# A deformable-convolution stack with a mixture-of-experts block: six gather buffers instead of ten, fourteen sample buffers instead of eight

## The chip, the cores and the metric

The kernel runs on one core of a Trainium2 chip. The metric is the device time of one execution in microseconds. TensorE is called PE here (PEld is its weight load), VectorE DVE, ScalarE ACT, GpSimd POOL and SyncE SP.

## What is computed

The input `x` is (4, 256, 64, 64) in float32. It is normalised over the channels and goes through three modulated deformable 3x3 convolutions with ReLU; the result is added to `x`. Each pixel's 256 channels then form a token that goes, normalised, through a mixture of eight experts (256 to 512 to 256, GELU), of which the two with the highest gate probability are taken, and is added again. One deformable convolution is, cut to what matters here:

```python
om = conv3x3(x, w_off) + b_off                 # 27 values per pixel
off, mask = om[:, :18].reshape(B, 9, 2, H, W), sigmoid(om[:, 18:])
ys, xs = gy + base_y + off[:, :, 0], gx + base_x + off[:, :, 1]
sampled = bilinear(x, ys, xs) * mask           # 4 corners per pixel and tap
out = einsum('bikhw,oik->bohw', sampled, w) + b
x = relu(out)
```

Each pixel and each of nine taps so reads four neighbouring pixels at a place that only the data know.

## The kernel before

**Work and stages.** Three layers times four images are twelve stages (`self.stages` in `run`). A stage has eight blocks of 512 pixels (`NB`), a block nine taps (`K`), and a tap four samples: a sample here is 128 pixels (one per partition) by 256 channels for one tap. There are 12 x 8 x 9 x 4 = 3456 samples. `main_block` loops over taps and, within a tap, over two pairs of samples.

**A sample's way.** For each layer and image a table lies in DRAM whose rows hold a pixel and the one below it, so that two neighbouring rows, 4 KB together, are the four corners. `samples` does four things for each sample, one on each engine:

- L503, POOL: an indirect DMA gathers 128 table rows of 4 KB into a tile `g` of pool `gat` (4 KB per partition). The row numbers `idx` come from a plan made earlier (`off_block`).
- L509, DVE: blends the two columns, in place in `g`.
- L514, DVE: blends the two rows into a tile `s` of pool `smp` (1 KB per partition). After it `g` is free.
- L517, ACT: scales `s` in place with the mask and weight.

`turn` then takes a pair of samples: PE transposes the two `s` into PSUM (L532), after which they are free, and ACT copies the result to `sT` (L535). After two pairs `finish` multiplies `sT` with the tap's weights and accumulates in `acc` (L555). `LAG = 2` keeps `turn` two pairs behind `samples` in the order in which instructions are recorded.

**Order and rings.** The recorded order goes through a scheduler which fixes each engine's order at build time; engines then run in that order and wait on semaphores. A tile of a pool can be written when all users of an earlier tile in the same buffer are done. So `gat`'s buffer count bounds how far POOL's gathers run ahead of DVE's second blend, and `smp`'s how far DVE's blends run ahead of PE's transposes. In the build of before, a gather waits for a blend of an earlier sample (the buffer) and for an earlier DMA of the software queue.

**Work beside.** Between taps other work is woven in on all engines. `off_block` makes offsets and plans (L357, L366, L371, L387 to L427). `pre_block` normalises the input of a later image (L442, L462, L467). `rows_done` and `store_table` write the next layer's table (L328, L338). `tokens`, `route` and `invert` prepare the FFN (L599 to L788: gate, ranks, slots; `at` and `num` at L777 and L779). `expert` runs an FFN tile: POOL fetches weights `w` (L800) and tokens `zt` (L812), PE transposes (L840) and multiplies (L856, L874), ACT copies (L844) and applies GELU (L866), `products` writes `y` with DVE (L892). `combine_fetch` and `combine` gather the experts' results `gy` (L915) and add them to `ta` on DVE (L930); `give` transposes and stores (L948 to L956). An FFN tile's steps are spaced by a pace of 5, 5, 2, 1.5 and 0 taps for the five groups of tokens.

**Other users of the gather buffers.** While the kernel starts, `room` takes the blocks `xc` and `h` of `pre_block` from the pool `gat`. The last FFN group takes its `gy` from it as well, after the last gather (`combine_fetch`).

Of the kernel before, what the change touches and what calls it, by code (L numbers as in the profile page):

```python
# [34 lines left out]
FT_LOG = 8  # L35
FT = 1 << FT_LOG
FU = FT // P
GB = 10
LAG = 2
LEAST = 2.0**-30  # L40
WINN = CC * (RPB + 2) * W
# [41 lines left out]
class Group:  # L83


    def __init__(self, b, n0, n1):
        self.b, self.n0, self.n1 = b, n0, n1
        self.nm = f"{b}_{n0}"
        self.M = (n1 - n0) * TPB

        self.NF = 2 * self.M * P // FT + E - 1


        self.half = (self.NF + 1) // 2
        self.zt, self.acc, self.gy, self.sums, self.py = {}, [], [], [], None
        self.order = [s // 2 + s % 2 * self.half for s in range(self.NF)]
# [21 lines left out]
class Weave:  # L118
# [3 lines left out]
    def __init__(self, ctx, tc, ins, out):  # L122
        nc = self.nc = tc.nc
        self.tc = tc
        self.ins = ins
        self.x = ins["x"].rearrange("b (c p) h w -> b p c (h w)", p=P)
        self.out_v = out.rearrange("b (c p) h w -> b p c (h w)", p=P)
        self.B = self.x.shape[0]

        def pool(name, bufs, **kw):  # L130
            return ctx.enter_context(tc.tile_pool(name=name, bufs=bufs, **kw))

        self.cst = pool("cst", 1)
        self.dram = pool("dram", 1, space=bass.MemoryType.DRAM)
        self.wkp = pool("wkp", 1)
        self.plan = pool("plan", 19)
        self.win = pool("win", 3)
        self.wt = pool("wt", 2)
        self.small = pool("small", 1)
        self.big = pool("big", 2)  # L140
        self.ffn = pool("ffn", 2)
        self.rt = pool("rt", 1)
        self.rt2 = pool("rt2", 2)
        self.gyp = pool("gyp", 4)
        self.smT = pool("smT", 2)
        self.smp = pool("smp", 8)
        self.gat = pool("gat", GB)
        self.ps = pool("ps", 3, space=bass.MemoryType.PSUM)
        self.ps1 = pool("ps1", 1, space=bass.MemoryType.PSUM)

        self.routes, self.tiles, self.sums = Lane(), Lane(), Lane()
        self.side, self.plans_side = [], []
        self.last = self.gathered = self.turned = None
        self.starting, self.draining, self.later = True, False, []
        self.pend, self.pairs = None, []
# [980 lines left out]
```

## Time and profile before

| | |
|---|---|
| median of 9 runs | 7635.78 us (7607.57 to 7649.76) |
| the profiled execution | 7654.8 us |
| its span | 7653.1 us, 88985 instructions |
| granted PE clock, mean | 0.937 |
| first and last gather issued | 94.0 us, 7194.3 us |
| bytes moved | 2223.73 MB, 291 GB/s in the mean |
| software queue (gathers, FFN fetches) | 1947.35 MB, 72.3% of 16 DMA engines' span |
| hardware queue (SP's loads and stores) | 270.69 MB, 10.7% |

The span is the time from the first to the last recorded instruction of the profiled execution. A row of the groups or the timeline names the line, the engine, the operation and the tiles, output first (`s<-g,cf`). A wait is idle time of an engine before an instruction, put down to what ended it; "issue" means that nothing in the profile ended it, and "remote" that the releaser was not found.

### The profile page before, as it was taken

The page shows a single profiled execution, that of the slowest core. Times are in us where ns is not written, and L with a number is a line of the kernel's source. Part 1 is how long each engine was busy: PE and PEld are TensorE (multiplying, and loading weights), DVE is VectorE, ACT ScalarE, POOL GpSimd, SP SyncE. Part 2 cuts the span into 40 slices and gives each one's busy share as a digit, 9 for nine tenths or more (in the row PEclk, how much of TensorE's full clock was granted, in tenths as well). Part 3 has the DMA queues.
Part 4 walks back from the last instruction along what each step waited for, and adds up shares of the span by engine and source line. Part 5 has one row for each costly group of instructions (what it writes and reads, how often), then busy time and mean ns, then how long its engine had stood idle before and what let it go on. Part 6 is the DMA issues. An engine that isn't in the chain of part 4 may idle for free.

```text
span 7653.1 us, 88985 instructions
## 1 busy us (share of the span) xinstructions
PE 6480.1 (85%) x26500; PEld 3640.5 (48%) x26500; DVE 4952.0 (65%) x11467; ACT 3266.2 (43%) x7141; POOL 4468.3 (58%) x4245
## 2 busy tenths in 40 slices
PE   7887888888898888889987888888888788977887
PEld 3443333334444444455554444544444455644565
DVE  6776777778886566567777556656767554667421
ACT  3444444444544444445443444444444333444322
POOL 4654666656666556556556656655655555566543
PEclk8999999999999999999998999999998899999888
DMA  8987999989999888888888889888887777888644
GB/s 270 337 315 269 345 324 338 344 324 354 353 344 315 291 298 294 285 299 314 302 296 306 285 280 317 298 290 296 294 301 281 253 256 240 275 293 287 202 134 125
DMA packets 800319, 2223.73 MB, mean 291 GB/s; under 512 B 104728, under 2 KB 302872, under 8 KB 794080
## 3 DMA queue, kind: packets, MB, share of 16 engines
q0 software_dynamic: 551200, 1947.35, 72.3%
q1 hardware_dynamic: 248640, 270.69, 10.7%
q8 instruction: 215, 3.52, 0.2%
q14 instruction: 264, 2.16, 0.1%
HBM read 2160.68 MB, written 196.40 MB: 308 GB/s over the span
## 4 chain that ended last, share of the span: by engine, by line
PE 67%; ACT 10%; another core or an unknown queue 8%; issue 7%; DVE 4%; DMA 2%; POOL 1%; SPq 0%; ACTq 0%; POOLq 0%; DVEq 0%
PE acc L555 33%; PE tp L532 10%; PE ph L856 7%; PE py L874 7%; PE po L357 6%; ACT sT L535 4%; ACT s L517 3%; DVE g L509 1%; PE pm L371 1%; DVE s L514 1%; ACT hT L866 1%; PE ftp L840 1%; PE lp_tok L618 1%; ACT win L577 1%
## 5 line engine op out<-in xcount | busy, mean ns | idle before, releaser
L503 POOL DMA_INDIRECT g<-tab,idx x3456 | 3679.4, 1065 | 2468.9 <-DVE s L514 1106.6
L555 PE MATMUL acc<-sT,wk 128*128 128x512 f32 x6912 | 3502.9, 622 | 272.0 <-ACT sT L535 147.2
L509 DVE SCALAR_TENSOR_TENSOR g<-g,cf 128x512 f32<-128x512 f32 x3456 | 2557.9, 742 | 261.5 <-DMA g<-tab,idx 243.2
L514 DVE SCALAR_TENSOR_TENSOR s<-g,cf 128x256 f32<-128x256 f32 x3456 | 1661.9, 483 | 1409.4 <-PE tp L532 746.3
L535 ACT COPY sT<-tp 128x512 f32<-128x512 f32 x1728 | 1001.9, 585 | 2416.6 <-PE tp L532 1576.9
L555 PEld LDWEIGHTS acc<-sT,wk 128*128 128x128 f32 x6912 | 1200.4, 198 | 1130.1 <-issue 831.3
L517 ACT ACTIVATE s<-s,cf 128x256 f32<-128x256 f32 x3456 | 1628.7, 508 | 242.7 <-DVE s L514 156.4
L532 PEld LDWEIGHTS tp<-ident,s 128*128 128x128 f32 x6912 | 897.2, 147 | 1715.1 <-issue 953.1
L532 PE MATMUL tp<-ident,s 128*128 128x128 f32 x6912 | 1291.1, 288 | 484.5 <-ACT s L517 269.7
L874 PE MATMUL py<-w,hT 128*128 128x256 f32 x2608 | 687.0, 403 | 139.7 <-ACT hT L866 84.7
L856 PE MATMUL ph<-fzT,w 128*128 128x256 f32 x2608 | 721.1, 411 | 67.3 <-ACT fzT L844 29.7
L874 PEld LDWEIGHTS py<-w,hT 128*128 128x128 f32 x2608 | 494.4, 200 | 282.0 <-ACT hT L866 123.1
L856 PEld LDWEIGHTS ph<-fzT,w 128*128 128x128 f32 x2608 | 507.9, 206 | 204.5 <-issue 68.2
L866 ACT ACTIVATE hT<-ph,w 128x256 f32<-128x256 f32 x652 | 281.9, 471 | 634.4 <-PE ph L856 372.9
L812 POOL DMA_INDIRECT zt<-z,tok x326 | 333.6, 1023 | 171.3 <-issue 87.7
L800 POOL DMA_INDIRECT w<-in_W,wrow x163 | 177.1, 1087 | 416.0 <-ACT sT L535 172.6
L357 PE MATMUL po<-win,wo 128*32 128x504 f32 (+1 forms) x2304 | 364.6, 609 | 6.7 <-ACT win L301 3.6
L892 DVE TENSOR_TENSOR y<-py,w 128x512 f32<-128x512 f32 x163 | 111.9, 686 | 377.8 <-PE py L874 314.0
L915 POOL DMA_INDIRECT gy<-ys,slots x256 | 254.5, 994 | 108.0 <-issue 71.8
L930 DVE SCALAR_TENSOR_TENSOR ta<-gy,cw,ta 128x256 f32<-128x256 f32 x256 | 120.4, 479 | 128.6 <-DMA gy<-ys,slots 76.0
L357 PE MATMUL po<-win_pre,wo 128*32 128x504 f32 (+1 forms) x1152 | 187.7, 628 | 2.0 <-ACT om L366 2.0
L366 ACT ACTIVATE om<-po,bo 128x512 f32<-128x512 f32 x96 | 66.0, 687 | 255.3 <-PE po L357 170.0
(154 smaller groups left out, 2968.5 us busy)
## 6 DMA issues: line engine op xcount, KB each, us to landing
tab<-hv SPq DMA_DIRECT2D x512, 128.0 KB
g<-tab,idx POOLq DMA_INDIRECT x3456
ys<-y SPq DMA_DIRECT2D x163, 256.0 KB
tab<-h_pre SPq DMA_DIRECT2D x128, 256.0 KB
wk<-in_conv_w SPq DMA_DIRECT2D x99, 256.0 KB
xc_pre<-in_x SPq DMA_DIRECT2D x32, 512.0 KB
xr_tok<-in_x SPq DMA_DIRECT2D x32, 512.0 KB
t<-t_tok SPq DMA_DIRECT2D x32, 512.0 KB
```

The source lines that it names most:

```text
L357: nc.tensor.matmul(po[g * Q : (g + 1) * Q, :].rearrange("q (r w) -> q r w", w=W)[:, :, x0:x1], lhsT=self.wo[l][:, 3 * ky + kx, c, :], rhs= ...
L503: self.gathered = nc.gpsimd.indirect_dma_start(out=g.rearrange("p x s f -> p (x s f)"), out_offset=None, in_=self.table(*self.stages[i]), ...
L509: nc.vector.scalar_tensor_tensor(g[:, :, 0, :], g[:, :, 1, :], cf[:, j, 0:1], g[:, :, 0, :], ALU.mult, ALU.add,)
L514: self.last = nc.vector.scalar_tensor_tensor(s, g[:, 1, 0, :], cf[:, j, 1:2], g[:, 0, 0, :], ALU.mult, ALU.add)
L517: nc.scalar.activation(s, s, AF.Copy, scale=cf[:, j, 2:3])
L532: self.turned = nc.tensor.transpose(tp[:, c, u * P : (u + 1) * P], ss[u][:, c * P : (c + 1) * P], self.ident)
L535: nc.scalar.copy(self.sT[:, :, t0 * P : (t0 + 2) * P], tp)
L555: nc.tensor.matmul(acc[:, o, :], lhsT=self.wk[k][:, c, o * P : (o + 1) * P], rhs=sT[:, c, :], start=(k == 0 and c == 0), stop=(k == K - 1 ...
L812: self.nc.gpsimd.indirect_dma_start(out=zt, out_offset=None, in_=grp.zd, in_offset=bass.IndirectOffsetOnAxis(ap=grp.tok[:, j : j + 1], axi ...
L856: nc.tensor.matmul(ph[:, h, :], lhsT=w1[:, o : o + P], rhs=zT[:, c, :], start=(c == 0), stop=(c == CC - 1),)
L866: nc.scalar.activation(ht[:, h, :], ph[:, h, :], AF.Gelu, bias=w1[:, k : k + 1])
L874: nc.tensor.matmul(py[:, u, :], lhsT=hT[h // 2][:, h % 2, u * P : (u + 1) * P], rhs=w2[:, h * C : (h + 1) * C], start=(h == 0), stop=(h == ...
```

## The change

The pool of gather tiles has six buffers instead of ten, and the pool of blended samples fourteen instead of eight. Per partition that is 16 KB less and 6 KB more. Nothing else is edited; the scheduler makes each engine's order anew.

```diff
-GB = 10
+GB = 6
...
-        self.smp = pool("smp", 8)
+        self.smp = pool("smp", 14)
         self.gat = pool("gat", GB)
```

## The prediction

> **What bounds the kernel now.** I read the busy times first, then the waits, then the instruction rows of single stretches.
>
> ```profile
> PE 6480.1 (85%) x26500; PEld 3640.5 (48%) x26500; DVE 4952.0 (65%) x11467; ACT 3266.2 (43%) x7141; POOL 4468.3 (58%) x4245
> ```
>
> PE is the busiest engine. The span of 7653.1 us is its 6480 us and about 1170 us of idle time; only a change that shortens this idle time or adds to it moves the end. Two of the waits look as if the change would act on them (columns: who waited for whom, us in total, times, longest):
>
> ```profile
> POOL g L503 <- DVE s L514: 1106.6, 646, 14.6
> DVE s L514 <- PE tp L532: 746.3, 616, 8.9
> DVE s L514 <- remote: 232.6, 101, 12.4
> ```
>
> They form a chain of full rings. POOL cannot gather because all ten `g` are held; DVE cannot free one because its blend needs a free `s`; the `s` are held until PE has transposed them. But these are waits of the engines that feed PE, and a feeder that waits for its customer is early. PE's own waits say what PE lacks:
>
> ```profile
> PE tp L532 <- ACT s L517: 269.7, 245, 15.4
> PE acc L555 <- ACT sT L535: 147.2, 167, 5.9
> ...
> ACT s L517 <- DVE s L514: 156.4, 167, 9.0
> ```
>
> PE waits for ACT, which scales a sample in place (L517) and copies the transposed pair (L535). ACT in turn waited for DVE's blend only 156.4 us.
>
> I then paired the rows by count: gathers, both blending operations, the scaling and the transposes run through the samples in one order, so the k-th row of L503, L509, L514 and L517 and the k-th two of L532 are the same sample. A gather's landing I took from the software queue's packets: each gather has 128 packets of 4 KB, and the end of the last is its landing, to a few tenths of a us. Three things come out.
>
> (a) A gather takes 5.2 us in the median from issue to landing (7.0 at the 95th percentile). Up to 6000 us the median gather finds ten buffers held at its issue, of which 3 to 4 are in flight and some six have landed and wait.
> (b) From landing to its blend a sample lies 10.2 us in the median, and from blend to transposition another 12.0 us; six blended samples are in stock when PE transposes one.
> (c) Of PE's idle time (1158 us in gaps over 0.1 us) 467 us stand before a transposition whose sample was blended before PE went idle, and 15.6 us, in ten gaps, before one that was not; of these 7.4 us are the first samples of all, which no buffer helps.
>
> So through most of the kernel the supply of samples is not what PE waits for. Two stretches are different. At the first gathers the rings are empty (start in us, duration, engine, line, operation, idle time before it):
>
> ```profile
> 93.98 1.02 POOL L503 DMA_INDIRECT g<-tab,idx  x1 [58.67 <-DMA tab<-h_pre]
> ...
> 96.59 0.94 POOL L503 DMA_INDIRECT g<-tab,idx  x1 [0.30 <-issue]
> 97.84 0.94 POOL L503 DMA_INDIRECT g<-tab,idx  x1 [0.30 <-issue]
> 98.00 0.75 DVE L509 SCALAR_TENSOR_TENSOR g<-g,cf 128x512 f32<-128x512 f32 x1 [10.49 <-DMA g<-tab,idx]
> 98.79 0.48 DVE L514 SCALAR_TENSOR_TENSOR s<-g,cf 128x256 f32<-128x256 f32 x1
> ...
> 104.31 0.75 DVE L509 SCALAR_TENSOR_TENSOR g<-g,cf 128x512 f32<-128x512 f32 x1
> ```
>
> The first gather is blended 4.0 us after its issue, the fourth (97.84) after 6.5 us. The other is 6000 to 7200 us, with an FFN tile every 1.5 to 2 taps (DVE's waits in that window):
>
> ```profile
> DVE g L509 <- DMA g<-tab,idx: 230.1, 75, 10.3
> ...
> DVE s L514 <- PE tp L532: 21.7, 9, 8.9
> ```
>
> Nearly all of DVE's 243.2 us for gathers lies there, and a full `s` ring hardly occurs. POOL is held there by the weight fetch at L800 (172.6 us behind `ACT sT L535` over the kernel), not by `g`: the median gather finds five buffers held, and only 29% more than six.
>
> **The change, part by part.** No instruction is added or removed in the computation. In the built programs the order of samples is the same, and few instructions change places: 31 on POOL, 91 on DVE, 442 on ACT (by six places at most), 531 on PE, nearly all of them in the second half of each engine's order.
>
> *Six g.* A buffer's turn is the landing (5.2 us), two blends (0.742 + 0.483 us by L509 and L514) and about 0.35 us until POOL starts again: 6.8 us, so six buffers allow one sample each 1.13 us. With the 7.0 us latency it is 8.6 / 6 = 1.43 us. POOL issues at best each 1.25 us (the rows at 96.59 and 97.84), and the kernel consumes one each 2.05 us ((7194.3 - 94.0) / 3456). Six is therefore enough in the steady state, by a factor of 1.8, and too few only for a fast catch-up on a loaded queue.
>
> One step finer: I hold every gather of before back to the end of the blend six earlier plus 0.3 us, with its own latency, and compare its landing with the time at which DVE blended it. The mean gather moves 6.2 us later, and 111 of 3456 blends become late, in 59 episodes whose longest lateness adds up to 67 us. Of this, 27 us are one episode at 5914 us, where POOL sits behind the first fetches of an FFN group; there the new order puts two or three gathers ahead of those fetches. The other 58 episodes are at most 2.8 us each, and in the twenty longest the samples had 2 to 19 us between blend and transposition. So 0 to +27 us reach PE; I take +12, between, since the reordering mends part. With five buffers the same count gives 613 late blends: six stands near an edge.
>
> *Fourteen s.* DVE's 979 us (746.3 + 232.6) of waiting for a free `s` shrink, but they stand on no path to PE by (b) and (c). What it can save: of the 15.6 us in (c) the 8 us after the start, and the part of ACT's 156.4 us that PE feels. ACT is idle 4387 us (span less busy), and PE's gaps behind a scaling that started late are 402 us, 9% of that; 9% of 156 is 14 us. Ends are 0 and 156; I take 14, for (c) says that the blend is rarely what ACT lacks. Together -22 us.
>
> A rule of the Trainium skill speaks otherwise: "Perfetto Trace Analysis", Identifying Performance Opportunities, says that the same gap repeating on an engine can mean too little memory for the next tile. DVE's gaps before L514 fit that picture, and by it up to 979 us would be at stake. But the page means the engine that should be saturated, and here that is PE, whose row asks for ACT.
>
> *Start and end.* At the start `room` takes the input and normalised blocks from the same `g` ring, so these have six buffers too; the build adds waits to ACT's copies and SP's loads. Their releases (stores two or three blocks older) are 15 to 20 us old in the rows before 90 us: 0, at most +7 us, the longest such wait there already (PE for `xc_pre`). At the end the last FFN group borrows five `g` for its first ten `gy` pairs; six are enough: 0.
>
> *Waits.* 289 gathers now wait on three semaphores instead of two, while the scalings shed 209 second waits; at 17 to 50 ns for such a row this is under 15 us on engines that are ahead: 0. What queues behind a held gather on POOL are the fetches `w`, `zt`, `gy`; they move with it. DVE reaches `ta` (L930) four blends after the gather that precedes its `gy`, so with six ahead there remain ten blends, 12.5 us, for a transfer of 5 to 7 us: hidden.
>
> The DMA price by the Trainium skill, "DMA: Bandwidth & Descriptors", Anatomy of one DMA, is an estimate of 2.0 + 0.524 MB / 436 GB/s = 3.2 us, which would make six buffers good for 0.8 us a sample and the late blends fewer. The packets show 5.2 us, and the measurement decides.
>
> Sum: -22 + 12 = -10 us, so 7645 us for an execution like the profiled one (7654.8 us) and 7626 us beside the median of 7635.8, which lies 19 us under the profiled time.
>
> **Rivals.** *Six is too few (slower).* DVE, freed from the `s` ring, runs to the edge of the landed gathers, and the loaded 1.43 us sets the pace whenever PE consumes faster. It decides from the point where the blended stock is empty when a late gather is awaited; the place is the stretch around 5000 to 6000 us, with 120 of the 164 us of summed lateness. For it: the edge at five. Against it: stock moves past DVE, and 14 + 6 is two samples deeper than 8 + 10. Price: all 67 us, 7703; beyond that only if lateness breeds lateness.
>
> *ACT's wait counts (faster).* If half of ACT's 156 us behind blends is felt by PE through the copies queued behind L517, 78 us go: 7558. For it: bursts in which FFN routing fills DVE (the `num` and `at` rows) drain the stock to 0 to 1. Against it: (c).
>
> **Numbers.** A measurement here can tell about 0.2% (15 us) from no change. Forecast case 0.55, its own range 7605 to 7650, mostly within 0.2% (0.37), else 0.13 faster and 0.05 slower; slower rival 0.25; faster rival 0.20. That gives faster 0.33, same 0.37, slower 0.30. The range reaches both rivals: 7560 to 7700.
>
> **What would show it.** Right: DVE's wait for PE before L514 falls well below 746 us, with POOL's wait for DVE still near 1100 us, while `PE tp <- ACT s` stays near 270 us and PE's idle time near 1160 us. `DVE g <- DMA g` may rise from 243 us to 300 or 400 us without harm. The slower rival shows as that row rising by several hundred us together with `ACT s <- DVE s` and PE's idle time; the faster one as `ACT s <- DVE s` falling below 80 us and PE's idle time by 70 us. I am wrong if PE's idle time moves by over 80 us either way.

## The result and the profile after

The changed kernel takes 7792.68 us (median of 10 runs, 7769.41 to 7822.55) against 7633.82 us for the kernel before (31 runs): a ratio of 1.021, 95% interval 1.0194 to 1.0225. The forecast was 7626 us within 7560 to 7700, so the kernel became slower by 159 us where a gain of about 10 us was forecast. The profiled execution took 7801.49 us, its span is 7799.8 us.

First the page's busy times, then the waits (columns: who waited for whom, us in total, times, longest):

```profile
PE 6535.6 (84%) x26500; PEld 3667.6 (47%) x26500; DVE 4998.7 (64%) x11467; ACT 3279.7 (42%) x7141; POOL 4456.9 (57%) x4245
```

```profile
ACT sT L535 <- PE tp L532: 1460.7, 879, 7.9
POOL g L503 <- DVE s L514: 1173.5, 535, 26.9
...
ACT sT L535 <- remote: 582.5, 119, 11.6
DVE g L509 <- DMA g<-tab,idx: 459.5, 361, 10.5
...
DVE s L514 <- PE tp L532: 299.9, 250, 6.9
ACT s L517 <- DVE s L514: 286.3, 272, 9.0
PE tp L532 <- ACT s L517: 268.6, 217, 10.5
...
DVE s L514 <- remote: 165.0, 60, 9.2
...
PE acc L555 <- ACT sT L535: 133.5, 149, 8.4
```

PE's span of 7799.8 us is 6535.6 busy and 1264.2 idle. Against before that is 55.5 us more busy time (granted clock 0.929 for 0.937) and 91.2 us more idle time, together the 146.7 us by which the span grew. The waits for rings behave as foreseen: DVE waits far less for a free `s` (299.9 for 746.3 us), more for landed gathers (459.5 for 243.2 us), and `PE tp <- ACT s` stays where it was (268.6 for 269.7 us). Two of ACT's rows grew by over 100 us. `ACT s <- DVE s` (156.4 to 286.3 us) is one that the prediction watched. The other it did not look at, and before it read:

```profile
ACT sT L535 <- remote: 472.9, 106, 13.4
```

"Remote" means that ACT, waiting for PE's transposes, stood on after these had ended by the trace. This row became the key to the case. All of ACT's "remote" rows together went from 844.7 to 935.7 us.

The prediction's measure (c), taken again on the changed kernel, tells which of the two PE felt: 532 us of PE's idle time (467 before) stand before a transposition whose sample was blended before PE went idle, and 27.5 us (15.6 before) before one that was not.

### The profile page after: what moved, and what is told of

It is laid out like the page before. It is cut to its first block, busy times and chain, and to the rows that moved or that the text cites. A ratio compares the mean times of both kernels' runs of the same rounds, so it can differ in the third digit from the quotient of the medians.

```text
span 7799.8 us, 88737 instructions
## 1 busy us (share of the span) xinstructions
PE 6535.6 (84%) x26500; PEld 3667.6 (47%) x26500; DVE 4998.7 (64%) x11467; ACT 3279.7 (42%) x7141; POOL 4456.9 (57%) x4245
## 4 chain that ended last, share of the span: by engine, by line
PE 59%; issue 10%; ACT 9%; another core or an unknown queue 8%; DVE 7%; DMA 5%; POOL 2%; SPq 0%; ACTq 0%; POOLq 0%; DVEq 0%
PE acc L555 28%; PE tp L532 9%; PE py L874 6%; PE ph L856 6%; PE po L357 5%; DMA g<-tab,idx 4%; ACT sT L535 3%; ACT s L517 3%; DVE g L509 2%; DVE s L514 2%; POOL g L503 1%; PE pm L371 1%; PE ftp L840 1%; ACT hT L866 1%
## 5 line engine op out<-in xcount | busy, mean ns | idle before, releaser
L503 POOL DMA_INDIRECT g<-tab,idx x3456 | 3662.8, 1060 | 2676.7 <-DVE s L514 1173.5
L509 DVE SCALAR_TENSOR_TENSOR g<-g,cf 128x512 f32<-128x512 f32 x3456 | 2564.9, 744 | 586.0 <-DMA g<-tab,idx 459.5
L514 DVE SCALAR_TENSOR_TENSOR s<-g,cf 128x256 f32<-128x256 f32 x3456 | 1662.3, 483 | 759.7 <-PE tp L532 299.9
L535 ACT COPY sT<-tp 128x512 f32<-128x512 f32 x1728 | 1002.5, 586 | 2524.0 <-PE tp L532 1460.7
L517 ACT ACTIVATE s<-s,cf 128x256 f32<-128x256 f32 x3456 | 1635.5, 508 | 375.1 <-DVE s L514 286.3
L532 PE MATMUL tp<-ident,s 128*128 128x128 f32 x6912 | 1302.0, 289 | 562.0 <-ACT s L517 268.6
L357 PE MATMUL po<-win,wo 128*32 128x504 f32 (+1 forms) x2304 | 368.4, 615 | 18.2 <-ACT om L366 9.3
L357 PE MATMUL po<-win_pre,wo 128*32 128x504 f32 (+1 forms) x1152 | 189.3, 636 | 2.0 <-ACT om L366 2.0
L366 ACT ACTIVATE om<-po,bo 128x512 f32<-128x512 f32 x96 | 66.0, 688 | 275.9 <-PE po L357 145.6
```

Source lines behind the costliest of these rows:

```text
L357: nc.tensor.matmul(po[g * Q : (g + 1) * Q, :].rearrange("q (r w) -> q r w", w=W)[:, :, x0:x1], lhsT=self.wo[l][:, 3 * ky + kx, c, :], rhs= ...
L503: self.gathered = nc.gpsimd.indirect_dma_start(out=g.rearrange("p x s f -> p (x s f)"), out_offset=None, in_=self.table(*self.stages[i]), ...
L509: nc.vector.scalar_tensor_tensor(g[:, :, 0, :], g[:, :, 1, :], cf[:, j, 0:1], g[:, :, 0, :], ALU.mult, ALU.add,)
L514: self.last = nc.vector.scalar_tensor_tensor(s, g[:, 1, 0, :], cf[:, j, 1:2], g[:, 0, 0, :], ALU.mult, ALU.add)
L517: nc.scalar.activation(s, s, AF.Copy, scale=cf[:, j, 2:3])
L532: self.turned = nc.tensor.transpose(tp[:, c, u * P : (u + 1) * P], ss[u][:, c * P : (c + 1) * P], self.ident)
```

## The experiments

The ratios below are each to the kernel before, run beside it.

**Which half of the change does it.** The edits are of one or two numbers:

```diff
-GB = 10                        # e1: 6   e2: 10   e3: 8   e4: 8
-self.smp = pool("smp", 8)      # e1: 8   e2: 14   e3: 8   e4: 14
```

Three theories stood at this point: A, six `g` are too few; B, fourteen `s` let DVE run ahead into waits of its own order; C, only the sum of both rings counts.

e1, six `g` alone: 

> Six gather buffers, eight sample buffers: only the first half of the change. If the short gather ring is the cause (theory A), it costs at least what the whole change costs: ratio to the kernel before 1.015 to 1.03, and DVE's wait for gathers well above 243 us. If the deep sample ring is the cause (theory B: DVE runs further ahead into waits of its own order), the ratio is 1.00 plus or minus 0.003. If only the sum of both rings counts (theory C: 14 samples of run-ahead instead of 18 here, 20 in the change), it is slower than the change itself, above 1.025.

Measured: 7407.88 us against 7508.32 us, ratio 0.9884 (0.9857 to 0.991). Fewer `g` are a gain.

e2, fourteen `s` alone: 

> Ten gather buffers, fourteen sample buffers: only the second half of the change. Theory A: 0.99 to 1.003, since the gather ring is as before and the added stock can only help. Theory B: about 1.02, with DVE's waits for L395 pos and L892 y grown as in the change. Theory C (24 samples of run-ahead): a gain of 0.5% or more.

Measured: 7973.43 us, ratio 1.0636 (1.0603 to 1.0669).

e3, eight and eight: 

> Eight and eight. Theory A: between, 1.002 to 1.010; counting lateness on the rows of before gave 40 us of late blends with eight buffers against 164 us with six. Theory B: 1.00. Theory C (16 samples): about 1.01.

Measured: 1.001 (0.9994 to 1.0027).

e4, eight `g` and fourteen `s`: 

> Eight and fourteen. Theory A: as eight and eight or up to 0.5% better, 0.997 to 1.010. Theory B: about 1.02. Theory C (22 samples): below 1.00.

Measured: 1.0582 (1.0551 to 1.0612). The fourteen `s` are the harm, and six `g` soften it (1.064, 1.058, 1.021 for ten, eight, six). A falls. So does C as "more depth helps". B has the right half, but not the size: it expected about 1.02 in e2 and e4, and no gain in e1. DVE's waits in e1:

```profile
DVE s L514 <- PE tp L532: 558.9, 494, 5.6
DVE g L509 <- DMA g<-tab,idx: 468.0, 381, 10.1
```

DVE waits as long for landed gathers as in the changed kernel, and the kernel is 1.2% faster: whatever this wait costs here is less than what six `g` gain.

**What a deep ring does.** The built programs of e2 and of before keep almost one order up to PE's last fifth, yet e2 loses steadily all along. In one order more buffers cannot make an instruction wait longer, so something outside the order had to change (this is an argument, not a measurement). ACT's waits, first in e1, then in e2:

```profile
ACT sT L535 <- remote: 374.9, 94, 9.9
```

```profile
ACT sT L535 <- remote: 735.6, 141, 13.6
...
ACT om L366 <- remote: 123.0, 11, 30.2
```

The longest, 30.2 us, is this stretch of e2 (timeline: start, duration, engine, line, operation, idle time before it):

```profile
4377.33 5.23 PE L357 MATMUL po<-win,wo 128*32 128x512 f32 x28
4382.49 0.65 PE L532 MATMUL tp<-ident,s 128*128 128x128 f32 x4
4382.98 1.02 PE L555 MATMUL acc<-sT,wk 128*128 128x512 f32 x2
...
4383.66 0.96 POOL L812 DMA_INDIRECT zt<-z,tok  x1 [0.30 <-issue]
...
4396.93 0.75 DVE L509 SCALAR_TENSOR_TENSOR g<-g,cf 128x512 f32<-128x512 f32 x1
...
4403.86 0.95 POOL L503 DMA_INDIRECT g<-tab,idx  x1 [0.30 <-issue]
4405.11 0.95 POOL L503 DMA_INDIRECT g<-tab,idx  x1 [0.30 <-issue]
4409.00 0.69 ACT L366 ACTIVATE om<-po,bo 128x512 f32<-128x512 f32 x1 [30.17 <-remote]
4409.10 0.48 DVE L514 SCALAR_TENSOR_TENSOR s<-g,cf 128x256 f32<-128x256 f32 x1 [11.42 <-remote]
4409.85 1.21 POOL L503 DMA_INDIRECT g<-tab,idx  x1 [3.80 <-DVE s L514]
4410.14 0.69 PE L532 MATMUL tp<-ident,s 128*128 128x128 f32 x2 [26.13 <-ACT s L517]
```

PE ended the offset convolution (L357) and four transposes by 4383.1. ACT waits for that convolution, DVE for a free `s` from those transposes, and PE itself for a scaling that is queued on ACT behind L366. All three stand until 4409. The trace also records when PE's signals (its semaphore increments) arrived: at 4408.98, 4409.02 and 4409.06. PE cannot run a convolution's last matmul and four transposes in 0.08 us (the four transposes alone took 0.65 us), so the work was done earlier and its signals were held, then let go in a clump. Meanwhile DVE blended into its free `s` and POOL issued one gather or fetch call after the other, until DVE's ring was full and POOL had no free `g`; its last call ended at 4406.06, and 2.9 us later the signals came.

I counted this in every trace: a late signal is one recorded over 1 us after the end of the newest matmul that could have sent it. PE has 562 of them in e2 and 418 in e1; ACT has 2 in each, DVE 8 and 2. In e2 1% of PE's signals are later than 7.9 us, in e1 than 4.5 us. Gathers are hardly slower: up to the first FFN fetch the median from issue to landing is 5.3 us in e2 and 5.2 us before.

From here the theories are: **D**, PE's signals are held while POOL issues gathers back to back, and a deep ring feeds such a row for longer; **E**, the backlog of transfers holds them; **B** as above; **F**, which only says that the harm of deep rings belongs to runs in which signals come late.

**Breaking up POOL's rows.** e5 and e12 are one kernel (ten `g`, fourteen `s`), e13 has it on six and eight:

```diff
+            if k % 2 == 0 and t == 0:
+                nc.gpsimd.memset(g, 0.0)      # e14, e15: twice
             self.gathered = nc.gpsimd.indirect_dma_start(
```

e5: 

> Ten g and fourteen s (ratio 1.064 without the edit), and once in about seven gathers GpSimd first overwrites the g buffer with zeros (a memset of 128x1024, then the gather fills it): GpSimd's rows of gathers are broken up, and nothing else is given or taken. Theory D (the matmul engine's signals come late while GpSimd issues gathers back to back; deep rings let it issue longer rows): ratio 1.00 to 1.04, and ACT's waits 'sT L535 <- remote' fall from 735.6 us to below 600 us. Theory E (it is the backlog of transfers that delays the signals, not GpSimd's issuing): the memsets take out 1 us in 9, the backlog stays: 1.05 to 1.07. Theory B (VectorE runs ahead into waits of its own order): the memsets only cost: 1.06 to 1.09.

Measured: 7154.71 us against 6806.0 us, 1.0516 (1.0494 to 1.0538). It answers none of the theories, because in e5 to e8, which ran together, nothing was held: two late PE signals in each trace, no "remote" row for ACT, and the kernel before took 6806 us. e17 and e18 ran later on the same chip and had late signals, so it is not the chip as such. What makes the difference I could not find out. How much of e5's 5.2% is the memsets and how much the fourteen `s` no run tells.

These runs do say one thing about D. Counting as one row all calls with less than 0.5 us between them, the longest row of e8 has 29 calls and that of before 30, e6 below has one of 201, and in e5 60% of the calls are in rows of eight or more; yet nothing was held in any of them. A row of calls alone is therefore not enough to hold them.

e6 and e7 halve the gathers' bytes (the blends are changed to read the one row twice):

```diff
-                out=g.rearrange("p x s f -> p (x s f)"),
+                out=g[:, 0, :, :].rearrange("p s f -> p (s f)"),
```

e6: 

> Ten g and fourteen s, and every gather brings 2 KB a partition instead of 4 KB (one of the two rows of four corners; the blend reads that row twice, so its instructions stay and the values of half of the corners are left out). GpSimd issues as many gathers as before. To be read against e7. Theory D: GpSimd's rows of calls are as long as ever, so fourteen s and ten g still lose to eight and six by 3% or more, and 'sT L535 <- remote' stays above 500 us. Theory E: with half the bytes the backlog is gone; e6 and e7 are within 1% of each other, 'sT L535 <- remote' is below 200 us in both, and both are below 0.95 of the kernel before. Theory B: e6 is slower than e7 by 3% or more, with 'sT L535 <- remote' small.

e7: 

> Six g and eight s with the same half gathers as e6. Theory D: 3% or more faster than e6. Theory E: within 1% of e6, and both below 0.95 of the kernel before. Theory B: 3% or more faster than e6.

Measured: 1.102 (1.1002 to 1.1039) and 1.1238 (1.1219 to 1.1257), far from all expectations. The scheduler orders the whole program differently (16544 of PE's 26500 matmuls stand elsewhere in e6 than in e10), probably because it takes a smaller gather to be cheaper, and DVE then waits for about every second gather. DVE's waits in e6:

```profile
DVE g L509 <- DMA g<-tab,idx: 1978.5, 1818, 9.6
```

With another order and prompt signals the pair says nothing of D against E.

e8, five `g`: 

> Five g and eight s, with whole gathers. Theories D and E (what counts is how far the gathers can run ahead of the transpositions, 13 samples here against 18 before): ratio 0.975 to 0.990. Theory B (only the depth of s matters, and fewer g make gathers late): 0.995 to 1.02.

Measured: 7143.26 us, 1.0496 (1.0479 to 1.0514), outside both ranges. ACT's and DVE's waits in e8:

```profile
ACT sT L535 <- PE tp L532: 1465.4, 1174, 5.1
ACT s L517 <- DVE s L514: 1083.8, 1074, 8.8
```

```profile
DVE g L509 <- DMA g<-tab,idx: 1248.9, 1283, 10.3
```

Here, where signals are prompt, ACT is short of blends and DVE of gathers, and five `g` cost what the prediction's slower rival feared. No run has five `g` with late signals, or six with prompt ones.

The next four ran together, with late signals again.

e9, the change once more: 

> The change itself once more, beside the next three on one chip. The traces so far are of two kinds. In those of before, after and e1 to e4 the matmul engine's signals come late (418 to 562 of them by over 1 us, the latest by 26 us); in those of e5 to e8, where the kernel before took 6806 us, 2 of them do. Theory F: the harm of deep rings is these late signals, and belongs to runs that show them. If they show here: 1.015 to 1.035. If signals are prompt here: fourteen s do nothing and six g make gathers late; e8 with five lost 5%, so six lose 1 to 4%. Theory B (VectorE in its own order, whatever the signals): 1.02 in both.

Measured: 1.0194 (1.0162 to 1.0227).

e10: 

> Ten g and fourteen s again. Theory F: with late signals 1.05 to 1.07; with prompt signals 0.985 to 1.005. Theory B: 1.05 to 1.07 in both.

Measured: 7982.86 us, 1.0631 (1.06 to 1.0662).

e11: 

> Six g and eight s again. Theory F: with late signals 0.98 to 0.995; with prompt signals 1.01 to 1.04, all of it waits of VectorE for landed gathers. Theory B: 0.985 to 1.00 in both.

Measured: 0.9877 (0.9845 to 0.9909). The three repeat e2, e1 and the change itself, as F has it for late signals. B's ranges hold as well, and F's other half, prompt signals, was not run, so these three do not separate the two.

e12: 

> e5 again, with e10 beside it: the memset ahead of one gather in seven breaks up GpSimd's rows of gathers. With late signals: theory D (the signals are held while GpSimd issues back to back) 1.00 to 1.04, against 1.05 to 1.07 for e10; theory E (the transfers' backlog holds them) within 1% of e10. With prompt signals both expect e5's 1.05, and e10 tells how much of that is the memsets.

Measured: 7762.0 us, 1.0335 (1.0291 to 1.0378). POOL has 480 memsets more to do, 465 us by e5's row, and the kernel is 221 us faster than e10. ACT's waits in e12, where two inserted lines shift L535 to L537, and for comparison in e10:

```profile
ACT sT L537 <- remote: 311.9, 76, 15.2
```

```profile
ACT sT L535 <- remote: 761.0, 142, 14.2
```

Late signals fall from 532 to 327. The rows of calls are shorter: 47% of POOL's calls are in rows of eight or more, against 67% in e10. The time speaks for D and against E and B. One reservation: the memsets also change the scheduler's order (PE's matmuls stand two places off in the median), and e12 against e10 is not free of that. e13 has nearly the order of e12, so these two can be compared without it.

e13: 

> Six g and eight s with the memset of e12 ahead of one gather in seven. Without memsets the two ring settings are 7.6% apart (1.0631 against 0.9877 with late signals). Theory D (signals are held during rows of gather calls; the deep rings' harm is their longer rows): with the pauses put in from outside the settings come within 4% of each other, so 0.995 to 1.03 here against e12's 1.0335. Theory B (the depth as such, through VectorE's order): still 6 to 8% apart, so 0.955 to 0.975. On a chip with prompt signals this is read against e5's 1.0516: at or above it, since six g make gathers late.

Measured: 0.9959 (0.9942 to 0.9976).

e14: 

> Ten g and fourteen s with two memsets ahead of one gather in seven: GpSimd's calls pause for some 2.5 us in place of 1.3. Held signals came 1 to 2.5 us after the last call, so theory D expects more of them let go in the pause: 'sT <- remote' below e12's 311.9 us, and at most 1.035 although GpSimd works some 480 us more. Theory B: above e12, 1.04 to 1.07.

Measured: 1.0396 (1.0356 to 1.0437), just above D's bound and just below B's range; 'sT <- remote' 234.7 us, as D has it. But late signals rose from 327 to 369, although only 25% of POOL's calls are still in rows of eight or more (47% in e12). That is against D.

e15: 

> Six g and eight s with two memsets. Theory D: e14 and e15 within 3% of each other, and this one at or above e13, since six g can't hide a pause of 2.5 us. Theory B: 6 to 8% faster than e14.

Measured: 1.0519 (1.0477 to 1.0561).

Deep against shallow rings: 1.0631 / 0.9877 = 1.076 without memsets, 1.0335 / 0.9959 = 1.038 with one, 1.0396 / 1.0519 = 0.988 with two. The more POOL's rows are broken up from outside, the less the depth costs, which D says and B does not. Neither pair with memsets is quite clean, since the pauses also make gathers late where there are six `g`. With one memset, DVE's wait for landed gathers is 740.0 us in e13 and 320.8 us in e12 (449.4 and 251.5 us in e11 and e10); with two it is 1669.6 us in e15 and 557.1 us in e14. So part of the narrowing is a loss of the shallow rings and not a gain of the deep ones. That e12 is faster than e10 is not touched by this.

**How it goes on with shallower rings.**

e16, six and six: 

> Six g and six s, no memsets: the gathers can run 12 samples ahead. Theory D: with late signals 0.975 to 0.99, below or at e11's 0.9877, unless VectorE now waits for s itself; with prompt signals 1.02 to 1.06. Theory B: 0.97 to 0.99 with either.

Measured: 0.983 (0.9793 to 0.9868), the fastest ratio of all that were run.

e17, eight and six: 

> Eight g and six s: the gathers can run 14 samples ahead, as in e11 (0.9877). If the run-ahead counts: 0.983 to 0.993. If the depth of s alone counts: as e16 or below, 0.970 to 0.983. With prompt signals (before near 6806 us): both 0.99 to 1.02.

Measured: 0.9963 (0.9946 to 0.998).

e18, ten and six: 

> Ten g and six s: run-ahead 16, as in e3 (1.001). If the run-ahead counts: 0.993 to 1.005. If the depth of s alone counts: 0.965 to 0.983. With prompt signals: both 0.99 to 1.02.

Measured: 0.992 (0.9897 to 0.9943). Neither rule fits: e17 lies above both ranges, e18 between them. Both rings have a share, and neither the sum nor `s` alone tells the time. The runs without memsets, all with late signals, from shallow to deep (they come from several chips and times; each ratio is to the kernel before run beside it, while the counts are of single traces):

| g + s | run | ratio | `ACT sT <- remote`, us | late PE signals |
|---|---|---|---|---|
| 6 + 6 | e16 | 0.983 | 385.6 | 417 |
| 6 + 8 | e1 | 0.988 | 374.9 | 418 |
| 8 + 6 | e17 | 0.996 | 448.6 | 455 |
| 8 + 8 | e3 | 1.001 | 403.0 | 434 |
| 10 + 6 | e18 | 0.992 | 383.8 | 415 |
| 10 + 8 | before | 1 | 472.9 | 485 |
| 6 + 14 | the change | 1.021 | 582.5 | 479 |
| 8 + 14 | e4 | 1.058 | 641.1 | 529 |
| 10 + 14 | e2 | 1.064 | 735.6 | 562 |

The counts follow the ratio at the deep end, but not for the change: it has 479 late signals where the kernel before has 485, and 57% of its calls are in rows of eight or more against 55% (67% in e2). ACT's waits follow better. All its "remote" rows together are 610 us in e11 (six and eight), 850 us in e9 (the change, on the same chip at the same time) and 1201 us in e10 (ten and fourteen).

## Why the prediction was wrong

**The step that failed** is "Fourteen s". It took DVE's 979 us of waiting for a free `s` as time that can only be saved or stay worthless, and gave the step the ends 0 and 156 us, taking 14 us as a gain with no end for a loss. Measured, fourteen `s` alone cost 6.4% (e2), and the wait was worth less than nothing. By theory D, which the memset runs support without proving it, it was what stopped DVE, then POOL, and so ended the holds of PE's signals: without it POOL goes on calling. The changed kernel escapes most of the cost, 2.1% against 6.4%; D's reason, that six `g` stop POOL earlier, is argued.

**A second term was put at nothing**: the prediction held PE's 6480 us of busy time fixed ("only a change that shortens this idle time or adds to it moves the end"). It grew by 55.5 of the 146.7 us. The granted clock was 0.929 for 0.937; no run separates what lowers it.

**Six g**, +12 us: the wait for landed gathers rose a little beyond what was foreseen, to 459.5 us ("300 or 400 us without harm"). Its harm by (c) stayed at some 12 us, and the part as a whole has the other sign: -1.2% (e1). By D that is because shorter rows of calls hold fewer signals (418 late ones in e1, 434 in e3, 485 before). No run tests the bound of 1.13 us a sample by itself.

**(b) and (c)**, that supply is not what PE lacks, hold: `PE tp <- ACT s` did not move, and of PE's idle time only 12 us more than before stand before a sample not yet blended, against 66 us more before one that was. But the prediction stopped at "PE waits for ACT" and did not ask for what ACT waits. ACT's longest single cause that the order does not explain was in the waits: `ACT sT L535 <- remote`, 472.9 us, and one line of the same kind was even shown, `DVE s L514 <- remote`.

**The rivals.** None named this. The slower one (late gathers) shows its marks in the changed kernel: the DMA row up by 216 us, `ACT s <- DVE s` up from 156.4 to 286.3 us, PE's idle time up. It is still not the cause, since e1 has the same DMA row and gains, and e2 has an unchanged one (251.1 us) and loses most. The faster rival's mark went the other way. The chance of 0.30 that the prediction gave to "slower" is no credit to it: 0.25 of that was for late gathers. **The test** set in advance, PE's idle time moving by over 80 us, was met with 91.2 us. Three of the four marks set for "right" came true all the same (299.9, 1173.5 and 268.6 us): they are waits of the rings, and do not test the step that failed.

**What stays open.** That a row of calls is what holds the signals rests on the memsets and on the moments of release, not on a mechanism that was seen. Against it stand e5, e6 and e8 (long rows, nothing held) and e14's late signals; if it holds, it needs a condition that was not found. In e10, of 92 clumps (two signals within 0.06 us after over 1 us without one) 54 came 1 to 2.5 us after the end of POOL's last call and 4 more than 3 us after it, although pauses of over 3 us take some 1500 us. POOL pauses also because it waits for these very signals, so this alone would prove nothing; in e12, 19 of 74 clumps came 0.5 to 2 us after the start of a memset, where 7 would by chance. E is weaker but not excluded: in e2, 2.5 gathers are still in flight when a clump comes, as at any moment (2.65); up to the first FFN fetch it is 3.6 against 3.0, over 17 clumps. The recording of the trace may have a part (last section). And neither the change nor fourteen `s` without memsets was run where signals are prompt, so whether the loss exists there is open.

## What to carry to other kernels

A wait of a feeding engine for a free buffer is not always worth nothing: it may be the brake that keeps a burst short. Give its removal an end on the side of loss, and try the shallower ring too. Where one engine's signals look late (a waiter that starts well after its releaser ended), compare that row between versions first: here it told more than any ring's wait. And a ratio found under one condition need not hold under another. Here all gains of shallow rings were measured with late signals, and with prompt ones five `g` lost 5%, so the gain of e16 should be measured there before it is kept.

## What the runs showed of the hardware that was not expected

- PE's completion signals arrived up to 26 us late in e2 and up to 29 us in e10, in clumps 0.04 us apart, while those of ACT and DVE in the same trace were on time (2 and 8 late ones in e2). In e2 95% of the engines so kept waiting started within 0.1 us of the recorded arrival, so the lateness is real time and not an error of the record.
- The same kernel, that of before, took 7508 to 7634 us beside the runs with late signals and 6806 us beside those without, a tenth less. Traces with late signals also lack records (in e1 4178 of PE's 5162 signals are there and 4879 of ACT's 6831; in e8 nearly all are), so recording itself may have a part in it; no run here separates the two.
- Rows of up to 201 gather calls with less than 0.5 us between them held no signals in e6.
- Adding 465 us of work to POOL, which also shifted the scheduler's order, made a kernel 221 us faster (e12 against e10).
